# A mixture-of-experts kernel's slot stage rebuilt: first layer transposed, copied weights, eight groups of batches instead of five

## The chip, the core and the metric

One core of a Trainium2 chip. The time is the device time of one execution in microseconds, the median of several runs; less is better. A profiled execution of each kernel gives the busy times, waits and timelines that are quoted.

## What is computed

One transformer block over x of 16 batches x 512 tokens x 128 channels, with adaptive layer norm: each batch has shifts, scales and gates (`sa, ca, ga, sb, cb, gb`) from a small product.

```
h = layernorm(x) * (1 + ca) + sa
x = x + ga * attention(h)          # 16 heads of 8, rope, causal mask
h = layernorm(x) * (1 + cb) + sb
x = x + gb * ffn(h)

ffn: logits = h @ router_w.T + expert_bias          # 160 experts
     probs = sigmoid(logits); top 8 per token
     w = 2.5 * top_w / (sum(top_w) + 1e-9)
     routed = sum over the token's 8 experts e of  w_e * silu(h @ w_gate[e].T) @ w_down[e].T
     shared = silu(h @ w_gate_shared.T) @ w_down_shared.T
     ffn = routed + shared                           # inner width 64
```

## The kernel before

The kernel has two stages. In the first, attention runs batch after batch, four groups of heads per batch (`attend`, 64 calls). Between its matmuls a list of small jobs (`Steps`) puts other work: preparing the next batches, and for a finished batch `project`, then `route` (layer norm, router logits, the top 8 of each token with MAX8 and MATCH_REPLACE8). When all batches of a *group* are routed, `place` gives each chosen (token, expert) pair a slot. Two experts share a *pair* of 128 hidden columns (2 x 64); there are `NC` = 80 pairs. The slots of a pair fill whole blocks of 128. A group of n batches gets `32 n + 80` blocks, so that there are always enough, and the last 8 quads of blocks (6 for a group of one batch) are spare: they run only when they are needed, behind a branch on all engines (`spare_quads`).

GpSimd then scatters the tokens' rows into the group's slots in HBM (`scattering`, indirect DMAs of 128 rows of 512 bytes, 32 per batch). The slots have been cleared before by DMAs from SyncE (`clear`, five in each `attend`).

In the second stage, `Quad` works on four blocks (512 slots) at a time, software pipelined over a loop whose order of stages is written by hand; every engine executes its instructions in that order:

- `load` brings the slots' rows `xs` from HBM, `turn` transposes them on TensorE into the PSUM tile `turn`, and ScalarE copies them to `xT`.
- `up` multiplies each block by its pair's gate weights, which lie in SBUF as `wg` (128 rows, 80 pairs of 128 columns and two router columns). The slots are the stationary operand, so the result has slots on partitions. Which of the pair's two experts a slot belongs to is a mask: a second product adds minus 1e30 (`away`) to the 64 columns of the other expert. ScalarE takes silu into `u` (tile `su`).
- The two router columns give the logit of the slot's expert once more. VectorE adds `shift` into `z`, and `begin_weights` and `end_weights` make the slot's unnormalised weight `w` of it, for two quads at a time, with one small silu (`sz`) on ScalarE.
- `back` transposes `u` again and VectorE copies it to `hT` (tile `hwT`); `down` multiplies by the down weights `wd`, loaded from HBM for each quad, and VectorE writes `y` = product times `w`. `y` goes to the slots' result `yg` in HBM.

Which pair a block belongs to is known only at run time. `numbers` loads the pair's numbers into registers (TENSOR_LOAD, line 768): in `load_down` on SyncE's queue, in `name_up` and `name_down` on TensorE's.

After a group's last quad GpSimd gathers for each block of 128 tokens the eight rows of `yg` (`gathering`, line 950: 8 indirect DMAs per 128 tokens, 32 per batch), and `combine` on VectorE adds the eight, multiplies by the token's normaliser `gr.scale` and by the gate, and adds to the residual `xr`, which already holds the shared expert (`shared_expert`).

Scatters and gathers are not issued freely: `Pacer` puts one at each `PACE_SLOTS` of the model time that `Steps` counts from the matmuls, and a manual dependency lets each wait for the matmul in front of it. `LAG` is the number of gathered blocks that may wait for `combine`; there are `LAG + 2` buffers `got`. Matmuls have line 104, transposes 111, and most VectorE and ScalarE instructions 1212, since helpers record them.

Of the kernel before, what the change touches and what calls it, by code (L numbers as in the profile page):

```python
# [35 lines left out]
GROUPS = (4, 4, 4, 3, 1)  # L36
TOPK = 8
FAR = 1e30
TINY = 1e-30
LAG = 4  # L40

PACE, PACE_SLOTS = 1.3, 0.9
# [28 lines left out]
def block_kernel(ctx: ExitStack, tc: tile.TileContext, t: dict, out: bass.AP):  # L71
# [88 lines left out]
    def load_rest():  # L160
        c.wrout = load("wroutT", [D, E])
        c.wgs = load("wgsT", [D, I])
        c.wds = load("wdsT", [I, D])
        c.bias_p = load("bias_p", [NC, 2])
        c.ones = load("ones", [P, 1])
        c.earlier = load("earlier", [P, P], BF)
        c.many = load("many", [1, P], BF)
        c.pairs = load("pairs", [NC, 2, NC])
        c.spread = load("spread", [NC, 2, E])
        c.table = load("table", [P, 2, NKM])  # L170
# [316 lines left out]
    rows = [tc.dram_tile([P, NBLK, D], FP, name=f"rows{b}") for b in range(NB)]  # L487

    somes = const.tile([1, len(GROUPS)], I32, tag="somes", name="somes")

    class Group:
        def __init__(self, g):
# [4 lines left out]
            self.scale = sb.tile([P, self.tb], FP, tag=f"scale{g}", name="scale")  # L497
            self.idx = sb.tile([P, self.tb, TOPK], I32, tag=f"idx{g}", name="idx")
            self.shift = sb.tile([P, self.nk, 2], FP, tag=f"shift{g}", name="shift")
            self.pid = sb.tile([1, self.nq, 9], I32, tag=f"pid{g}", name="pid")  # L500
            self.some = somes[:, g : g + 1]
            self.away = sb.tile(
                [P, -(-2 * self.nk // P), P], BF, tag=f"away{g}", name="away"
            )
            self.m, self.before = [], []
            self.xg = tc.dram_tile([self.nk * P, D], FP, name=f"xg{g}")
# [13 lines left out]
    def route(gr, i):  # L520
# [40 lines left out]
        yield  # L561

        top = sb.tile([P, NBLK, TOPK], FP, tag="top", name="top")
        for j in range(NBLK):
            vec.max(top[:, j, :], key[:, j, :])
            vec.match_replace(
                out=key[:, j, :], in_to_replace=top[:, j, :], in_values=key[:, j, :], imm_value=1.0
            )
            if j % 2:
                yield  # L570
        m = sb.tile([P, NBLK, E], BF, tag="m", name="m", bufs=max(GROUPS) + 2)
        vec.tensor_scalar(m, key, 0.0, None, ALU.is_gt)
# [13 lines left out]
        yield  # L586

        rs = gr.scale[:, i * NBLK : (i + 1) * NBLK]
        vec.reciprocal(top, top)
        vec.tensor_reduce(rs, top, AX.X, ALU.add, negate=True)  # L590
        vec.tensor_scalar(rs, rs, TOPK_EPS, None, ALU.add)
        vec.reciprocal(rs, rs)
        vec.tensor_scalar(rs, rs, ROUTED, None, ALU.mult)

    def place(gr):
# [41 lines left out]

# [58 lines left out]
        lim = gr.shift[:, :nk, :]  # L696
# [6 lines left out]
        vec.tensor_scalar(lim, lim, 1.0, FAR, ALU.subtract, ALU.mult)  # L703

        flat = tmp([P, 2 * NKM], BF, "flat")[:, : 2 * nk]
        vec.tensor_copy(flat, lim.rearrange("p n a -> p (n a)"))
        yield "o"
        pa = bank([P, -(-2 * NKM // P) * P], BF)
        for n, c0 in enumerate(range(0, 2 * nk, P)):
            k = min(P, 2 * nk - c0)  # L710
            turned(pa[:k, n * P : (n + 1) * P], flat[:, c0 : c0 + k], c.identb)
            vec.tensor_copy(gr.away[:k, n, :], pa[:k, n * P : (n + 1) * P])
        yield "o"
        for a in range(2):
            pl = bank([P, nk])
            mm(pl, c.bias_p[:, a : a + 1].broadcast_to([NC, P]), of)
            vec.tensor_tensor(lim[:, :, a], pl, lim[:, :, a], ALU.add)
            yield "o"
# [40 lines left out]
    class Quad:  # L759
# [17 lines left out]
        ALONE = {"xs": "a", "xT": "b", "su": "a", "wd": "c", "hwT": "b", "y": "a"}  # L777
# [11 lines left out]

        def load_down(self):  # L790
            (p0,) = self.numbers(SP, 0, 1, NC - 4)
            self.wd = self.tile([P, 4, D], "wd", 5)
            nc.sync.dma_start(out=self.wd, in_=t["wdT"][:, bass.ds(p0, 4), :])

        def turn(self):
            pt = now.ps.tile([P, S], FP, tag="turn", name="turn")
# [5 lines left out]
        def name_up(self):  # L802
            self.pids = self.numbers(PE, 1, 4, NC - 1)

        def up(self):

            pu = bank2().rearrange("p a (j n) -> p (a j) n", j=2)
            for j in range(4):
                mm(
                    pu[:, j, 0 : P + 2],  # L810
                    self.xT[:, j * P : (j + 1) * P],
                    wg[:, bass.ds(self.pids[j], 1), :].rearrange("p o n -> p (o n)"),
                    j % 2 == 0,
                    False,
                )
                n, k = divmod(4 * self.q + j, P // 2)
                rows_ = min(P, 2 * self.gr.nk - n * P)
                mm(
                    pu[:, j, 0:P].rearrange("p (a i) -> p a i", a=2),
                    self.gr.away[:rows_, n, :],  # L820
                    c.identb[:rows_, 2 * k : 2 * k + 2].unsqueeze(2).broadcast_to([rows_, 2, I]),
                    False,
                    j % 2 == 1,
                )

            if self.alone or self.q % 2 == 0:
                self.z = self.tile([P, 2, 4, 2], "z", 3)
            else:
                self.z = self.other.z
            vec.tensor_tensor(  # L830
                self.z[:, self.q % 2],
                pu[:, :, P : P + 2],
                self.gr.shift[:, 4 * self.q : 4 * self.q + 4, :],
                ALU.add,
            )
            self.u = self.tile([P, 4, P], "su", 3)
            act.activation(self.u, pu[:, :, 0:P], AF.Silu)

        def begin_weights(self):

            if self.q % 2 == 0 and not self.alone:
                return
            of = slice(self.q % 2, self.q % 2 + 1) if self.alone else slice(0, 2)
            z = self.tile([P, 2, 4], "z1", 3)
            self.w = self.tile([P, 2, 4], "w", 4)
            if not self.alone:
                self.other.w = self.w
            self.s = self.tile([P, 2, 4], "sz", 3)
            z, w = z[:, of], self.w[:, of]
            vec.tensor_tensor(z, self.z[:, of, :, 0], self.z[:, of, :, 1], ALU.max)  # L850
            vec.tensor_scalar(w, z, 0.0, TINY, ALU.is_equal, ALU.mult)
            vec.tensor_tensor(z, z, w, ALU.add)
            vec.reciprocal(w, z)
            act.activation(self.s[:, of], z, AF.Silu)

        def end_weights(self):
            if self.q % 2 or self.alone:
                of = slice(self.q % 2, self.q % 2 + 1) if self.alone else slice(0, 2)
                vec.tensor_tensor(self.w[:, of], self.w[:, of], self.s[:, of], ALU.mult)

        def back(self):
            pt = now.ps.tile([P, S], FP, tag="back", name="back")
            for j in range(4):
                turned(pt[:, j * P : (j + 1) * P], self.u[:, j, :], c.ident)
            self.hT = self.tile([P, S], "hwT", 3)
            vec.tensor_copy(self.hT, pt)
# [4 lines left out]
        def down(self):  # L871
            py = now.ps.tile([P, S], FP, tag="down", name="down")
            for j in range(4):
                mm(
                    py[:, j * D : (j + 1) * D],
                    self.hT[:, j * P : (j + 1) * P],
# [3 lines left out]
            vec.tensor_tensor(  # L880
                y,
                py.rearrange("p (n d) -> p n d", d=D),
                self.w[:, self.q % 2].unsqueeze(2).broadcast_to([P, 4, D]),
                ALU.mult,
            )
# [4 lines left out]
    def spare_quads(gr):  # L890
# [5 lines left out]
        with tc.If(some != 0):  # L896
            for q in range(gr.nq - spare(gr.size), gr.nq):
                quad = Quad(gr, q)
                quad.alone = True
                for stage in ("load", "load_down", "turn", "name_up", "up", "name_down"):  # L900
                    getattr(quad, stage)()
                quad.begin_weights()
# [509 lines left out]
```

## Time and profile before

| what | value |
|---|---|
| median of 3 runs | 1918.97 us (1918.86 to 1922.9) |
| profiled execution | 1925.86 us |
| its span | 1924.1 us |
| mean granted TensorE clock | 0.934 |
| busy: PE, PE weight loads, DVE, ACT, POOL | 1584.2, 1133.7, 1253.8, 826.6, 1117.9 us |
| first and last `turn` of a quad | 974.0, 1794.7 us |
| first scatter, first gather, last gather | 411, 1228, 1915.5 us |

The busy times are sums over the whole span; the stages have different limits, so windows and waits of the slot stage (from 974 us) count for this change. GB/s and the DMA share are means over 16 DMA engines. In a group of instructions, "out<-in" names the tiles.

### The profile page before, as it was taken

How to read it: one execution, taken by the hardware profiler on the slowest of the kernel's cores; microseconds unless marked ns; L12 is line 12 of the kernel's file. 1: busy time of each engine (PE TensorE's matmuls, PEld its weight loads, DVE VectorE, ACT ScalarE, POOL GpSimd, SP SyncE). 2: the span in 40 equal slices, each digit the busy share in tenths (PEclk: the TensorE clock that was granted, in tenths of full speed). 3: DMA queues.
4: the chain of work that ended last, by engine and by line, in shares of the span. 5: the costliest groups of instructions: out<-in, count | busy, mean ns of one | idle time of the engine just before them, and what ended most of it. 6: DMA issues, size and time to landing. Idle time of an engine off the chain costs nothing. (4 is left out here: it accounts for less than half of the span.)

```text
span 1924.1 us, 38397 instructions
## 1 busy us (share of the span) xinstructions
PE 1584.2 (82%) x12683; PEld 1133.7 (59%) x12747; DVE 1253.8 (65%) x3325; ACT 826.6 (43%) x1366; POOL 1117.9 (58%) x1139
## 2 busy tenths in 40 slices
PE   2799999998999989999888887888898878878700
PEld 1355555554555545555468776777788777777600
DVE  2677888887788867787636554546576656666622
ACT  1366666655666556664544332333233323323100
POOL 4001111047775477845657476777777777777776
PEclk8799999998999999999999898999899989999855
DMA  2456555565676667843257676778688878878622
GB/s 83 105 175 201 170 174 170 163 197 177 191 234 188 199 192 219 262 127 117 77 185 244 197 251 203 240 246 275 214 266 272 258 225 272 255 251 254 196 58 57
DMA packets 246678, 377.03 MB, mean 196 GB/s; under 512 B 37604, under 2 KB 136261, under 8 KB 246469
## 3 DMA queue, kind: packets, MB, share of 16 engines
q1 hardware_dynamic: 213700, 307.17, 51.4%
q0 software_dynamic: 32768, 67.17, 12.1%
q8 instruction: 119, 1.95, 0.4%
q14 instruction: 91, 0.74, 0.1%
HBM read 195.15 MB, written 178.26 MB: 194 GB/s over the span
## 5 line engine op out<-in xcount | busy, mean ns | idle before, releaser
L741 POOL DMA_INDIRECT xg<-hs,idx x512 | 493.4, 964 | 284.5 <-issue 95.0
L950 POOL DMA_INDIRECT got<-yg,idx x512 | 491.5, 960 | 156.7 <-issue 123.5
L1212 DVE TENSOR_REDUCE mins<-s 128x2 f32<-128x1024 f32 (+3 forms) x448 | 395.9, 913 | 123.5 <-PE s L104 121.7
L1212 ACT ACTIVATE pT<-s 128x1024 f32<-128x1024 f32 x320 | 323.0, 1021 | 176.7 <-PE s L104 172.3
L104 PE MATMUL s<-wg,xT 128*128 x1520 | 279.6, 307 | 0.6 <-issue 0.6
L104 PEld LDWEIGHTS s<-wg,xT 128*128 128x128 f32 x1520 | 241.6, 200 | 11.3 <-issue 1.2
L111 PE MATMUL turn<-ident,xs 128*128 128x128 f32 x760 | 123.8, 287 | 121.8 <-issue 49.7
L104 PE MATMUL s<-krep,qrep 96*128 96x512 bf16 (+3 forms) x1024 | 197.8, 306 | 31.9 <-DMA qrep<-parts 19.0
L104 PE MATMUL down<-wd,hwT 128*128 x1520 | 206.6, 280 | 3.7 <-DVE y L1212 3.7
L235 POOL TENSOR_TENSOR rot<-rot,three 128x512 f32<-128x512 f32 x32 | 36.8, 1160 | 291.4 <-ACT three L1212 289.4
L104 PE MATMUL s<-qrep,krep 128*128 128x128 bf16 (+3 forms) x960 | 181.6, 299 | 25.3 <-DVE mins L1212 12.3
L104 PE MATMUL av<-pT,v 128*32 128x512 f32 (+3 forms) x2048 | 193.4, 449 | 0.0
L104 PEld LDWEIGHTS down<-wd,hwT 128*128 128x128 f32 x1520 | 190.8, 197 | 4.1 <-DVE y L1212 4.0
L1212 ACT COPY xT<-turn 128x512 f32<-128x512 f32 x190 | 109.8, 578 | 164.8 <-PE turn L111 161.8
L111 PEld LDWEIGHTS turn<-ident,xs 128*128 128x128 f32 x760 | 85.6, 145 | 156.8 <-issue 116.4
L1212 DVE TENSOR_TENSOR z<-s,shift 128x8 f32<-128x8 f32 x190 | 29.6, 156 | 219.3 <-PE s L104 206.5
L104 PEld LDWEIGHTS <-identb 128*128 128x128 bf16 x1280 | 122.0, 100 | 84.9 <-issue 7.0
L104 PE MATMUL s<-identb,away 128*128 128x128 bf16 (+1 forms) x760 | 171.2, 225 | 0.0
L1212 ACT ACTIVATE su<-s 128x512 f32<-128x512 f32 x190 | 113.6, 598 | 129.3 <-DVE z L1212 121.8
L1212 DVE COPY hwT<-back 128x512 f32<-128x512 f32 x190 | 131.0, 689 | 44.2 <-PE back L111 43.6
L1212 DVE TENSOR_TENSOR y<-down,w 128x512 f32<-128x512 f32 x190 | 131.2, 691 | 38.5 <-PE down L104 33.6
L104 PEld LDWEIGHTS <-qrep 96*128 96x128 bf16 x1024 | 83.6, 99 | 119.7 <-issue 95.5
(179 smaller groups left out, 2356.6 us busy)
## 6 DMA issues: line engine op xcount, KB each, us to landing
xg<-zeros SPq DMA_DIRECT2D x228, 256.0 KB
xs<-xg SPq DMA_DIRECT2D x190, 256.0 KB
wd<-in_wdT SPq DMA_DIRECT2D x190, 256.0 KB
yg<-y SPq DMA_DIRECT2D x190, 256.0 KB
krep<-parts SPq DMA_DIRECT2D x64, 288.0 KB
qrep<-parts SPq DMA_DIRECT2D x192, 96.0 KB
parts<-three SPq DMA_DIRECT2D x96, 128.0 KB
yg<-zeros SPq DMA_DIRECT2D x38, 256.0 KB
```

The source lines that it names most:

```text
L104: steps.last = nc.tensor.matmul(out_, lhsT=lhsT, rhs=rhs, start=start, stop=stop).ins
L111: steps.last = nc.tensor.transpose(out_, in_, ident).ins
L235: in_order(getattr(nc.gpsimd, op)(*args).ins)
L741: s = nc.gpsimd.indirect_dma_start(out=gr.xg, out_offset=bass.IndirectOffsetOnAxis(ap=gr.idx[:, NBLK * i + j, k : k + 1], axis=0), in_=h[: ...
L950: s = nc.gpsimd.indirect_dma_start(out=got[:, k, :], out_offset=None, in_=gr.yg, in_offset=bass.IndirectOffsetOnAxis(ap=gr.idx[:, NBLK * i ...
L1212: return getattr(self.engine, op)(*args, **kwargs)
```

## The change

- `GROUPS` goes from (4, 4, 4, 3, 1) to (2, 3, 3, 2, 2, 2, 1, 1), `LAG` from 4 to 3, `PACE_SLOTS` from 0.9 to 0.75.
- `up` has the operands exchanged: the gate weights are stationary and `xT` moves, so the result comes with hidden columns on partitions, as `down` wants it. `back` and `hT` go.
- The stationary weights are copied first: `fetch_up` copies the four blocks' 128x128 weights from `wg` to `wq`, two on ScalarE and two on VectorE, each engine after a register load of its own. `name_up` goes from TensorE.
- The mask is one product per quad: a constant of two rows (`half`) times two rows of the quad's 512 slots (`hide`), which `place` writes to HBM and `load_hide` brings back for two quads at a time.
- The slots' weights go (`z`, `w`, `sz`, `shift`, `away`, the router columns of `wg`). Instead `route` stores the tokens' sigmoid keys and the mask of the chosen eight in HBM (`keys`, `chosen`). In the slot stage a new job `weights(b)` per batch loads them and gives each token's eight weights, in the order of the gathered rows: it builds sortable numbers from the expert's number and 16 bits of the key, takes MAX8, and does so again for the other 16 bits.
- `y` is a plain copy on ScalarE, and `combine` multiplies the eight gathered rows by the weights before it adds them.
- The PSUM banks: `turn` and `up` two each, `down` one; the loop is two turns shorter.

```
-GROUPS = (4, 4, 4, 3, 1)
+GROUPS = (2, 3, 3, 2, 2, 2, 1, 1)
-LAG = 4
-PACE, PACE_SLOTS = 1.3, 0.9
+LAG = 3
+PACE, PACE_SLOTS = 1.3, 0.75
...
         act.activation(key, key, AF.Identity, bias=minus, scale=-1.0)
         yield
+        nc.sync.dma_start(out=keys[b], in_=key)
...
+        nc.sync.dma_start(out=chosen[b], in_=m)
...
+            hide = sb.tile([P, P], BF, tag="hide", name="hide", bufs=2)
+            vec.tensor_copy(hide[:k], pa[:k, n * P : (n + 1) * P])
+            for a in range(2):
+                nc.sync.dma_start(
+                    out=gr.hide[a, c0 * I : (c0 + k) * I].rearrange("(n s) -> n s", s=P),
+                    in_=hide[a:k:2],
+                )
...
+        def fetch_up(self):
+
+            self.wq = self.tile([P, 4, P], "wq", 3)
+            for engine, copy, at in (
+                (mybir.EngineType.Activation, act.copy, 0),
+                (mybir.EngineType.DVE, vec.tensor_copy, 2),
+            ):
+                for j, pid in enumerate(self.numbers(engine, 1 + at, 2, NC - 1), at):
+                    copy(
+                        self.wq[:, j, :], wg[:, bass.ds(pid, 1), :].rearrange("p o n -> p (o n)")
+                    )
...
-            pu = bank2().rearrange("p a (j n) -> p (a j) n", j=2)
+            pu = now.ps.tile([P, S], FP, tag="up", name="up", bufs=2)
             for j in range(4):
+                to = pu[:, j * P : (j + 1) * P]
                 mm(
-                    pu[:, j, 0 : P + 2],
+                    to,
+                    self.wq[:, j, :],
                     self.xT[:, j * P : (j + 1) * P],
-                    wg[:, bass.ds(self.pids[j], 1), :].rearrange("p o n -> p (o n)"),
-                    j % 2 == 0,
+                    j == 0,
                     False,
                 )
...
+            mm(pu, c.half, self.hide, False, True)
+            self.u = self.tile([P, S], "su", 3)
+            act.activation(self.u, pu, AF.Silu)
...
-            vec.tensor_tensor(
-                y,
-                py.rearrange("p (n d) -> p n d", d=D),
-                self.w[:, self.q % 2].unsqueeze(2).broadcast_to([P, 4, D]),
-                ALU.mult,
-            )
+            act.copy(y.rearrange("p n d -> p (n d)"), py)
...
+    def weights(b):
+        while len(weighed) < weighing.index(b):
+            yield
+        key = moe.sb.tile([P, NBLK, E], FP, tag="wkey", name="wkey")
+        nc.sync.dma_start(out=key, in_=keys[b])
+        m = moe.sb.tile([P, NBLK, E], BF, tag="wm", name="wm")
+        nc.sync.dma_start(out=m, in_=chosen[b])
+        yield LATER
+        base = moe.sb.tile([P, NBLK, E], FP, tag="base", name="base")
+        vec.tensor_tensor(base, m, c.high.unsqueeze(1).broadcast_to([P, NBLK, E]), ALU.mult)
...
+        for n, (by, mask) in enumerate(((16, 0x7FFF), (0, 0xFFFF))):
+            vec.tensor_scalar(digit, bits, by, mask, ALU.logical_shift_right, ALU.bitwise_and)
+            vec.tensor_tensor(both, base, digit, ALU.add)
+            yield
+            for j in range(NBLK):
+                vec.max(eight[:, n, j, :], both[:, j, :])
...
+        vec.tensor_tensor(
+            got, got, w[:, j, :].unsqueeze(2).broadcast_to([P, TOPK, D]), ALU.mult
+        )
         for n in (4, 2, 1):
             vec.tensor_tensor(got[:, 0:n, :], got[:, 0:n, :], got[:, n : 2 * n, :], ALU.add)
...
-    for i in range(-3, len(quads) + 7):
+    for i in range(-3, len(quads) + 5):
         for stage, q in (
             ("load", i + 3),
-            ("load_down", i - 3),
-            ("name_up", i - 1),
-            ("name_down", i - 5),
-            ("end_weights", i - 4),
-            ("begin_weights", i - 3),
+            ("load_hide", i),
+            ("load_down", i - 1),
+            ("fetch_up", i),
             ("turn", i),
             ("up", i - 2),
-            ("back", i - 4),
-            ("down", i - 6),
+            ("name_down", i - 3),
+            ("down", i - 4),
```

## The prediction

> **What bounds the kernel now.** I read the page's slices first, then windows over the slot stage, the engines' timeline of one quad, and last the waits.
>
> ```profile
> span 1924.1 us, 38397 instructions
> POOL 4001111047775477845657476777777777777776
> DMA  2456555565676667843257676778688878878622
> ```
>
> Up to about 974 us the kernel does attention (TensorE nearly always busy), from there the slots, from 1815 us only gathers. GpSimd starts to scatter in the ninth slice and is busy at 7 of 10 from slice 25 to the end.
>
> ```profile
> 1000.00:1010.00 10.00, 10.00 (x71) 7.72 (x70) 3.81 (x11) 5.03 (x8) 7.56 (x9) 1.00 0.96 331
> ...
> 1400.00:1500.00 100.00, 87.85 (x752) 81.19 (x750) 71.80 (x203) 35.09 (x73) 76.15 (x79) 1.00 0.86 273
> ...
> 1800.00:1850.00 50.00, 15.43 (x88) 11.82 (x87) 21.50 (x52) 2.67 (x6) 38.11 (x40) 0.63 0.42 122
> 1850.00:1900.00 50.00, 0.00 (x0) 0.00 (x0) 10.98 (x27) 0.00 (x0) 37.81 (x41) 0.50 0.23 58
> ```
>
> The columns after the time are PE, PE's weight loads, DVE, ACT and POOL, then clock, DMA share and GB/s. GpSimd issues about 79 to 80 gathers in 100 us with work beside it and 41 in 50 us with none: one per 1.25 us (0.94 busy, 0.30 between) is its natural rate. DMA can go to 331 GB/s for 10 us and has held 273 for 100 us.
>
> ```profile
> 1523.00 0.63 PE L111 MATMUL turn<-ident,xs 128*128 128x128 f32 x4 [0.81 <-ACT su L1212]
> 1523.46 0.39 PE L104 MATMUL s<-wg,xT 128*128 x2
> ...
> 1524.75 0.61 PE L111 MATMUL back<-ident,su 128*128 128x128 f32 x4
> ...
> 1525.19 1.06 PE L104 MATMUL down<-wd,hwT 128*128 x8
> ...
> 1526.08 0.60 PE L111 MATMUL turn<-ident,xs 128*128 128x128 f32 x4
> ```
>
> From start to start a quad costs TensorE 0.46 (turn) + 1.29 (up with masks) + 0.44 (back) + 0.89 (down) = 3.08 us. The 190 quads, however, take (1815 - 974) / 190 = 4.43 us each. The waits say where the rest goes:
>
> ```profile
> ACT sz L1212 <- DVE z L1212: 206.4, 88, 7.8
> PEld turn L111 <- issue: 116.4, 96, 6.9
> ...
> L768 PEldq TENSOR_LOAD <-pid x380: 332/1004/2452, 974.0 to 1807.9; - x190
> ...
> L892 ACTq TENSOR_LOAD <-somes x5: 278/479/756, 1186.2 to 1811.1; - x5
> L892 DVEq TENSOR_LOAD <-somes x5: 304/312/555, 1187.3 to 1815.9; - x5
> ```
>
> ScalarE stands in `sz` behind VectorE's weights and combines, so the next `xT` leaves the only `turn` bank late; and TensorE's sequencer loads block numbers twice per quad, 1.0 us each, more than its queued matmuls always cover. So the slot stage is bound by a chain PE, DVE, ACT with GpSimd close to full beside it, and the end by the gathers left over: (1924 - 1815) = 109 us.
>
> **The change, part by part.** All sums are against the profiled execution (span 1924.1, 1925.9 with what lies around it); the median shown, 1919.0, lies 7 us lower, so 7 is taken off at the end.
>
> *Number of quads.* A group of n batches has 32n + 80 blocks, so 8n + 20 quads, less 8 spare ones (6 for n = 1). Before: 44 + 44 + 44 + 36 + 22 = 190. After: 28, 36, 36, 28, 28, 28, 22, 22 = 228. That is 38 quads more, at any price.
>
> *TensorE per quad.* `back` goes (0.44). Up takes down's form, four fp32 products of 128 columns: 0.89; the eight mask instructions become one bf16 product of 512 columns (0.22 at the 128-column masks' rate of 0.055). Sum 0.46 + 0.89 + 0.22 + 0.89 = 2.46. One of two register loads remains, 1.0 us, covered by the down matmuls queued behind the sequencer; uncovered it costs what two did now, some 0.5. The shared expert (about 2.6 us per batch, 16 / 228) adds 0.18; at the stage's mean clock of 0.95 (the windows' clock column, averaged) that is 2.64 / 0.95 = 2.78 us.
>
> *ScalarE per quad.* Out: `sz` (0.21 per two). In: `y` and two weight copies. The profile's rows:
>
> ```profile
> L1212 ACT COPY xT<-turn 128x512 f32<-128x512 f32 x190 | 109.8, 578 | 164.8 <-PE turn L111 161.8
> L1212 ACT ACTIVATE su<-s 128x512 f32<-128x512 f32 x190 | 113.6, 598 | 129.3 <-DVE z L1212 121.8 <-ACT xT L1212 4.5 <-DVE w L1212 1.5
> ```
>
> 0.578 + 0.598 + 0.58 for `y` + two copies. No copy of 128x128 from SBUF is in the trace: the nearest row is `gate` (PSUM source) at 265 ns, the upper bound the normalisation's 128-column rows at 483. I take 0.27. The sum is 2.30 us, plus a register load of 0.48 (0.28 to 0.76) that starts while `y` still runs: 2.3 to 2.8.
>
> *VectorE.* Out per quad: `z` 0.16, five small ones (0.44), `hwT` 0.69, `y` 0.69. In: two copies (0.22 to 0.30 each by `away` and `xr<-xr,got`), 0.5 taken. In per batch: four products of 1024 columns, 1.22 each from the rows' slope, 4.9; and `weights`, two casts-and-adds of 640 columns and eight MAX8 at 0.32, about 8 us. With the old combine's 8.3 and the shared expert's 1, 22 us per batch: 2.0 us per quad in all, below TensorE, but in lumps of 3 us in front of the weight copies. Up uses these two turns later, which covers 5 us.
>
> *DMA.* Each quad moves 3 x 256 KB. 228 quads 179 MB, some 100 scatters left plus 512 gathers at 64 KB 40 MB, per batch 3 x 256 KB + 480 KB (`keys`, `chosen`) 20 MB: 239 MB. At 300 GB/s, between the 273 held and the 331 seen, 797 us. The Trainium skill ("SBUF — State Buffer", A bandwidth-pool intuition that's wrong) gives 358 GB/s from HBM to a core; by it 668 us, and DMA would not bind. The trace holds less already at a share of 0.96, so I take 300.
>
> *GpSimd.* About 100 scatters and 512 gathers at 1.25 us are 765 us after the switch. The skill's rule ("SBUF — State Buffer", SBUF: two separate sides) speaks against the change: VectorE's fp32 copies within SBUF lock the port through which GpSimd writes its descriptors. By the rule 456 copies of 0.25 could add up to 114 us. The row: a gather's median is 944 ns and its mean 960 with the `got` sums beside it, 2%, or 15 us. I take 15 and keep the 114 for the range.
>
> *SP.* `load_hide` is one issue per two quads; `keys` and `chosen` are two in and two out per batch at 0.4, and wait for ACT's `key` and DVE's `m` with q/k fetches queued behind them, four groups ahead; cost taken as nothing, and a few us a batch if that lead is gone. Clears grow from 266 to 348. Five per attention group go (320), so 28 are left for the switch: 28 x 0.38 = 11 us of SP ahead of the first `xs`.
>
> *Attention.* Three more placings, smaller masks, no scale: -5 to +20, +5 taken. With the clears the first turn is at 990 instead of 974.
>
> *Spare blocks.* Each branch makes its quad 9.6 to 10.4 us long instead of 3.8, and the clock is halved after it: 8 us. Seven lie inside the stage: 56 (before four).
>
> *Tail.* After the last down, 32 gathers: 3.5 + 40 + 9 (as now from the last gather) + 1.5 = 54 instead of 109, provided GpSimd has no backlog. It hasn't: by the seventh group's end, about 1715, it has had time for 580 of the 548 due.
>
> *Sum.* Bytes give (797 - 56) / 233 turns = 3.18 us, TensorE 2.78, ScalarE 2.3 to 2.8, GpSimd 780 / 233 = 3.35 with branches' time included, 3.1 without. Where four are this close no one of them runs free, so 3.25. 990 + 233 x 3.25 + 56 + 54 = 1857, median 1850. Equal to now at X = (1924 - 1100) / 233 = 3.54.
>
> **The rivals.**
>
> *GpSimd is the floor.* The quads run at 2.8 as TensorE alone allows: 990 + 652 + 56 + 54 = 1752, and GpSimd ends at 990 + 780 + 9 = 1779; median 1772. For it: no DMA wait among the SP's. Against it: 239 MB in 710 us is 337 GB/s, more than the best ten microseconds of now.
>
> *ScalarE becomes the serial engine: slower.* Its queue takes all of a quad's evacuations in order, and now a register load and two copies ahead of `xT`. If the load isn't hidden (0.76), copies cost 0.48 and each of five waits 0.06, the turn is 0.76 + 0.97 + 1.76 + 0.30 = 3.8 us: 990 + 885 + 56 + 54 = 1985, median 1978. It decides from 3.54. For it: `y` has only two buffers and needs `yg` to land while DMA is at 0.9. Against: a load of this kind began 25 ns after `su` did and ran beside it. DMA sustaining under 271 GB/s ends at the same place.
>
> *The gain is eaten by quads alone.* The chain through VectorE was not what cost 4.43, X stays at 3.54: 1924, no change.
>
> **How the numbers follow.** 3.05 to 3.45 per turn has 0.45 (1803 to 1897); GpSimd's floor 0.20; 3.45 to 3.52 0.08; no change 0.04; slower 0.23. So faster 0.73, same 0.04, slower 0.23. A difference under 0.2% can't be told here from none. The range 1768 to 1955 leaves out the best of the second case and the worst of the slow one; the likeliest case alone is 1803 to 1897.
>
> **What would show it.** Right: 228 `xT` at 3.2 to 3.3 us, no `back`, DMA at 290 to 310 GB/s over the slot stage, last down near 1800 and 32 to 40 gathers after it, first gather near 1100 instead of 1228, first scatter near 290 instead of 411. Wrong: ScalarE above 85% in the slot stage or `y` waiting for `yg` (the slower rival); TensorE idle for `wq` from VectorE (its lumps); gathers above 1.3 us each (the port rule); the first turn after 1010.

## The result, and the profile after

The changed kernel takes 1993.34 us (median of 4 runs, 1989.1 to 1997.8) against 1918.91 for the kernel before: a ratio of 1.0385 [1.0356, 1.0415], so it is slower, and the prediction of 1850 us has the wrong sign. The profiled execution has a span of 1993.5 us, 69 more than before.

Two rows of the changed kernel's page, the busy tenths of GpSimd and DMA in 40 slices:

```profile
POOL 4001117713775567766736757677777774757636
...
DMA  3456646756766676667688688888787888888871
```

GpSimd begins two slices earlier than before (first scatter at 304 us instead of 411), but then it is not steadily at 7: it has holes (a 3 in slice 21, a 4 and a 5 in slices 34 and 36, a 3 in slice 39), where the kernel before shows 7 in nearly every slice of the last third. The windows (PE, weight loads, DVE, ACT, POOL, then clock, DMA share, GB/s):

```profile
1400.00:1500.00 100.00, 78.46 (x503) 64.87 (x503) 56.24 (x158) 50.56 (x116) 77.13 (x76) 0.88 0.78 249
1700.00:1800.00 100.00, 87.76 (x605) 74.17 (x606) 53.00 (x154) 60.22 (x142) 63.70 (x64) 0.91 0.87 285
1950.00:1993.00 43.00, 0.00 (x0) 0.00 (x0) 12.87 (x24) 0.00 (x0) 26.43 (x28) 0.50 0.19 50
```

In the first, GpSimd gathers back to back and TensorE is at 78%, at a clock of 0.88; in the second TensorE does better and GpSimd issues only 64 gathers. The first turn of the quads comes at 1022 us instead of 974, the last down at 1940 instead of 1815, and the tail after it is 53 us.

Of the waits of the stage of quads (engine, line, what was waited for: us in total, times, longest):

```profile
DVE got L1217 <- DMA got<-yg,idx: 62.1, 21, 6.8
POOL got L961 <- SPq L861: 60.6, 3, 26.4
...
PE o L110 <- DMA hr<-rows: 33.6, 7, 6.5
...
PE up L103 <- DMA hides<-hide: 24.6, 14, 3.0
PE up L103 <- DVE wq L1217: 24.6, 14, 5.4
PE turn L110 <- DMA xs<-xg: 23.5, 3, 21.3
```

VectorE waits for gathered rows, TensorE for weight copies on VectorE and for loads that come late (`hr` of the shared expert, the mask's `hides`), and GpSimd stands three times for up to 26 us at the branch of the spare blocks (L861), with nothing to gather. SyncE, which issues the loads, stands 78 us in front of the store `out`, which waits for `combine`:

```profile
SPq L985 <- DVE xr L1217: 77.7, 14, 11.9
```

One case in which these waits hang together: `combine` waits 2.8 us for gathered rows and begins at 1418.6, the copies to `wq` stand behind it on VectorE, and SyncE stands from 1411 to 1422 in front of `out`, with `hides` behind it. TensorE meanwhile:

```profile
1422.79 1.22 PE L103 MATMUL up<-xT,wq 128*128 128x128 f32 x4 [3.41 <-DVE wq L1217]
1425.94 0.58 PE L103 MATMUL up<-hides,half 2*128 2x512 bf16 x1 [1.94 <-DMA hides<-hide]
...
1429.14 1.06 PE L110 MATMUL turn<-ident,xs 128*128 128x128 f32 x4
1429.99 1.92 PE L103 MATMUL up<-xT,wq 128*128 128x128 f32 x8
```

From 1422.8, at the end of the first of these waits, to 1433.0 the granted clock is 0.5. And one of GpSimd's holes:

```profile
1917.87 0.95 POOL L961 DMA_INDIRECT got<-yg,idx  x1 [0.30 <-PE down L103]
1945.23 0.94 POOL L961 DMA_INDIRECT got<-yg,idx  x1 [26.42 <-SPq L861]
```

A group's gathers exist only when its last quad and its branch are through. GpSimd had emptied its list before that, and the next gather comes right behind the branch.

**An account by GpSimd's line.** From the traces: the time of the first turn, the scatters then left and the 512 gathers at 1.25 us each (the median from start to start in these runs), GpSimd's idle time between them (each distance over 2 us, less 1.25), and as the rest the wait for the first of them, the short gaps and some 8 us behind the last gather:

| run | first turn | scatters left | (scatters + 512) x 1.25 | idle | rest | end |
|---|---|---|---|---|---|---|
| before | 974 | 197 | 886 | 34 | 30 | 1924.1 |
| after | 1022 | 142 | 818 | 119 | 35 | 1993.5 |
| e16 (pace, stores, clears) | 1002 | 142 | 818 | 38 | 40 | 1898.2 |
| e17 (the same, old groups) | 974 | 195 | 884 | 48 | 43 | 1948.7 |
| e18 (the same, 3, 4, 4, 4, 1) | 991 | 196 | 885 | 87 | 35 | 1998.7 |

Such a sum comes out for any engine; it tells something here because little of it is idle time. In the kernel before GpSimd idles for 34 of 950 us behind the first turn, so that its line, and not the quads, sets the end. In the changed kernel the quads set it in part, through the 119 us in which GpSimd waits for them. The change puts 55 more scatters under attention (-69 us), comes 48 us later to the first turn, and lets GpSimd stand 85 us longer: that and 5 us of rest are the 69 us.

And TensorE's side, the stage from first turn to last down, cut into idle (gaps over 0.15 us), what the halved clock costs (half of the busy time in stretches of granted clock 0.5), and the rest, its own work at full clock:

| run | stage | quads | idle | halved clock | own work | per quad |
|---|---|---|---|---|---|---|
| before | 842 | 190 | 135 | 32 | 674 | 3.55 |
| after | 919 | 228 | 149 | 65 | 705 | 3.09 |
| e16 | 834 | 228 | 92 | 36 | 706 | 3.10 |
| e17 | 671 | 190 | 62 | 27 | 582 | 3.07 |

A quad is 13% cheaper, but there are 20% more of them.

### The profile page after: what moved, and what is told of

Read it like the earlier page. It is cut to its first block, busy times and chain, and to the rows that moved or that the text cites. A ratio compares the mean times of both kernels' runs of the same rounds, so it can differ in the third digit from the quotient of the medians.

```text
span 1993.5 us, 39230 instructions
## 1 busy us (share of the span) xinstructions
PE 1650.2 (83%) x12248; PEld 1129.7 (57%) x12248; DVE 1188.0 (60%) x3153; ACT 1080.0 (54%) x2031; POOL 1144.1 (57%) x1139
## 5 line engine op out<-in xcount | busy, mean ns | idle before, releaser
L103 PE MATMUL down<-wd,su 128*128 x1824 | 280.0, 300 | 30.5 <-DMA yg<-y 5.9
L103 PEld LDWEIGHTS down<-wd,su 128*128 128x128 f32 x1824 | 236.2, 202 | 114.3 <-issue 51.6
L103 PE MATMUL up<-xT,wq 128*128 128x128 f32 x1824 | 268.5, 293 | 31.1 <-DVE wq L1217 24.6
L103 PEld LDWEIGHTS up<-xT,wq 128*128 128x128 f32 x1824 | 245.8, 208 | 34.7 <-DVE wq L1217 27.6
L1217 ACT COPY y<-down 128x512 f32<-128x512 f32 x228 | 133.5, 586 | 184.4 <-PE down L103 121.4
L1217 DVE COPY wq<-wg 128x128 f32 x456 | 92.2, 250 | 235.4 <-PE up L103 146.6
L103 PE MATMUL s<-qrep,krep 128*128 128x512 bf16 (+3 forms) x1024 | 194.8, 303 | 33.5 <-DVE mins L1217 13.0
L1217 ACT ACTIVATE su<-up 128x512 f32<-128x512 f32 x228 | 136.3, 598 | 99.6 <-PE up L103 98.7
L1217 DVE TENSOR_TENSOR got<-got,w 128x1024 f32<-128x1024 f32 x64 | 78.3, 1224 | 99.3 <-DMA got<-yg,idx 96.2
L1217 ACT COPY wq<-wg 128x128 f32 x456 | 114.2, 296 | 40.8 <-issue 11.9
```

What stands on the lines that cost most here:

```text
L103: steps.last = nc.tensor.matmul(out_, lhsT=lhsT, rhs=rhs, start=start, stop=stop).ins
L1217: return getattr(self.engine, op)(*args, **kwargs)
```

## The experiments

E1 to E12 ran on three chips (E1 to E4, E5 to E8 and E9 to E12 on one each) on which the kernel before takes 2195 to 2199 us, below called the slower chips; the result above and E13 to E18 are from faster chips, on which it takes 1919 to 1920. Each ratio is to runs of the kernel before on the same chip. Edits are shown shortened.

**E1 to E4: pace, the store of the output, clears, groups, one at a time.** Theory Q was: one gather per 0.75 us of planned time asks for more than GpSimd gives; combines on VectorE and the store `out` on SyncE then stand in front of copies and loads.

```
-PACE, PACE_SLOTS = 1.3, 0.75                # E1, again as E7
+PACE, PACE_SLOTS = 1.3, 1.1
-   if j == NBLK - 1: nc.sync.dma_start(out=out[b]..., in_=xr)    # E2
+   if j == NBLK - 1: late_outs.append((turn + 6, b, xr))         #  issued six turns later
-   if n % 3 == 1 and clears:                # E3
+   if (n % 3 == 1 or n == 6) and clears:
-GROUPS = (2, 3, 3, 2, 2, 2, 1, 1)           # E4
+GROUPS = (4, 4, 4, 3, 1)
```

> Only PACE_SLOTS goes from 0.75 to 1.1. Theory Q (queues behind the gathers): the program asks for a gather about every 0.8 us, GpSimd gives one per 1.25, so `combine` on VectorE waits for rows, and the weight copies on VectorE and `out` on SyncE's queue stand behind it. Slower pacing takes the backlog away: VectorE's waits for `got` in the slot stage fall from 62 us to under 20, SyncE's for `xr` from 78 to under 25, the slot stage (first turn to last down) from 919 us to 820 to 850; more gathers are left for the end, time 1920 to 1960. Theory D (the bytes of 228 quads): the slot stage stays over 890 us, since as much is moved, and the tail grows: 2000 to 2040. Theory S (ScalarE serial): as D.

> `out` of a batch is issued on SyncE's queue six turns of the loop later, nothing else. Theory Q: SyncE no longer waits for `xr` (78 us to under 10), loads are not late and TensorE's waits for `hr`, `xs` and `hides` (33.6, 23.5 and 24.6 us) fall to under half, but the weight copies still stand behind `combine`: slot stage 919 to 870 to 895, time 1945 to 1975. Theories D and S: SyncE's order does not matter, 1983 to 2003.

> Six clears in each attention group instead of five, so that none of the 28 is left for the switch. If they delay the first slots' loads: first turn from 1022 to 998 to 1005, TensorE's wait for `xs` there (21 us) gone, time 1970 to 1980. Rival: the clears cost the attention stage what they save at the switch (DMA or SyncE time in both), first turn within 5 us of 1022, time 1985 to 2000.

> The changed kernel with the groups of before, (4, 4, 4, 3, 1): 190 quads instead of 228. If the new quad is good and the groups lost the time: first turn under 1000, 190 quads at 4.0 us or less, but 64 us later first gather; GpSimd then ends at about first gather 1230 + 640 + 9: 1880 to 1930. If the new quad itself lost it (theories D, S): 190 quads over 4.4 us and over 1950.

Measured, ratios to before with their 95% intervals: E1 0.9953 [0.9932, 0.9974], E2 1.0717 [1.0670, 1.0763], E3 1.0634 [1.0589, 1.0679], E4 1.0146 [1.0098, 1.0195]. Against the unaltered change (E5, 1.0753) the later output store gives nothing that counts. The times expected were for a faster chip; as shares of E5, E1 gains more than Q gave it (2 to 4%), E2 as little as D and S said, E3 and E4 what was expected of the clears and of the groups. E3 brings the first turn to 1093 us, where E1 and E2 on the same chip have 1109 and 1105 (the last clear is issued at 1009 instead of 1104 and 1100), and gains about 1%. E4 has its first turn at 1048 (before, on a chip as slow: 1056): the later start comes from the groups. The pace is the largest single term here (E1 is 7.4% under E5), and the groups are the second: taken back at the old pace (E4) they gain 5.6%.

**E5 to E8: the unaltered change as control, and three ways to take a queue out of the path.**

```
-   xr, gate, w = residual[b]                # E6: combine works on a fixed tile of zeros
+   xr, gate, w = residual[b]; got = still   #     (leaves out the use of the gathered rows;
                                             #     one gather tile fewer)
-   for engine, copy, at in ((Activation, act.copy, 0), (DVE, vec.tensor_copy, 2)):     # E8
-       for j, pid in enumerate(self.numbers(engine, 1 + at, 2, NC - 1), at): copy(...)
+   for j, pid in enumerate(self.numbers(Activation, 1, 4, NC - 1)): act.copy(...)
```

> The changed kernel unaltered, as the control for the other runs of this call. Its ratio to the kernel before was 1.0385 with 1993 us, and its stage of quads lasted 919 us (1022 to 1940). Theory Q (combines and stores queue behind gathers that are late) says nothing new here; both theories expect a ratio of 1.03 to 1.05. If the chip of this call is as slow as that of the first experiments (2195 us for the kernel before), the ratio should lie between those of the runs with only the store or the clears moved (1.063 to 1.072) and 1.04.

> Leaves out that the combine uses the gathered rows: it multiplies and sums a fixed tile of zeros instead, with the same instructions of the same sizes, while all 512 gathers still run (four gather tiles instead of five). So VectorE never waits for a gather, and the store of a batch never waits for one either. Theory Q: most of the stalls vanish; TensorE's idle time in the slot stage falls from about 149 us to 60 to 80 and the stage from 919 to 830 to 850 us, the total to 0.95 to 0.98 of the kernel before. Theory D (228 quads move too many bytes, 256 KB three times each, which DMA can't carry faster): the stage keeps 890 us or more, ratio 1.02 to 1.04. Theory S (ScalarE's serial queue): also unchanged.

> As the first experiment, a gather asked for per 1.1 us of planned time instead of 0.75, now beside the unaltered changed kernel on one chip. Q: fewer stalls in the stage but more gathers left at the end, net 3 to 5% faster than the changed kernel, ratio to before 0.98 to 1.01. D and S: gathers are only moved to the end, so it is slower than the changed kernel by 1 to 3%.

> All four weight copies of a quad on ScalarE, so nothing of VectorE lies between a quad's turn and its up products. Q: up's waits for the copies (about 52 us in TensorE's two rows) go, ScalarE rises by 2 x 0.30 us per quad (137 us, to about 70 to 75% busy), VectorE still stands behind gathers but only the store, the shared expert and the weights are late; stage 870 to 910 us, 1 to 4% faster than the changed kernel. S: ScalarE becomes the bound, 0.6 us per turn more, 137 us longer stage, ratio to before 1.10. D: no change.

Measured: E5 1.0753 [1.0729, 1.0777], E6 1.0719 [1.0695, 1.0743], E7 0.9924 [0.9896, 0.9952], E8 1.0843 [1.0813, 1.0872]. E5 is above all that was expected of it: the change loses more on the slower chips. Theory Q falls there: nothing waits for a gathered row in E6, and the stage is 1186 us instead of 1195. In E8 neither Q's gain nor S's 1.10 came. E7 repeats E1: 7.7% against E5, more than Q gave it, with the same 622 scatters and gathers inside the stage and 53 us behind it. So it isn't that gathers were moved to the end. GpSimd's idle time, by the account above, falls from 397 to 205 us with the pace; with the clears (E3) or the stores (E12) moved it stays at 378 and 384. Counted in blocks of eight turns in which GpSimd has no holes, E5 has about 4 gathers and scatters per turn and turns of about 6 us, E7 about 3 and 4.5. The turn grows with the number of gathers that the pace puts beside it.

How it looks there, in E6's timeline:

```profile
1733.71 0.38 PE L103 MATMUL up<-hides,half 2*128 2x512 bf16 x1
...
1743.37 0.94 POOL L962 DMA_INDIRECT got<-yg,idx  x1 [0.30 <-issue]
1745.48 0.36 DVE L1221 COPY wq<-wg 128x128 f32 x2 [9.73 <-remote]
...
1746.82 0.60 ACT L1221 ACTIVATE su<-up 128x512 f32<-128x512 f32 x1 [10.68 <-remote]
...
1747.95 0.80 PE L103 MATMUL down<-wd,su 128*128 x2 [13.85 <-ACT y L1221]
```

`su` needs only the product that ended near 1734.1 (the profile models the ends of matmuls), and begins 12.7 us later; TensorE, VectorE and ScalarE all stand while GpSimd issues gather after gather, and go on when its row of gathers is over. The profile names nothing as the releaser ("remote"). Two of E5's waits of this kind:

```profile
DVE wq L1217 <- remote: 151.9, 30, 12.0
...
ACT su L1217 <- remote: 133.1, 29, 8.7
```

This is not what happens in the result. In the slot stage ScalarE, VectorE and GpSimd wait 645 us for "remote" in E5, 147 in E7 and 179 in the kernel before (E9), all on slower chips; in the result, in the kernel before on its chip and in E13 to E18 it is not there once. On the other hand VectorE's waits for gathered rows, 62 us in the result's stage and 0.5 in that of the kernel before, are 0.7 us in E5: E6 took away a wait that was not there. So it excludes theory Q for the slower chips only, and the 7.7% is the worth of the pace on them.

**E9 to E12: where the slower chips lose, the quads without gathers, and the stores.**

```
-pacer = Pacer(PACE_SLOTS, scatter, gather)  # E10 (after) and E11 (before)
+pacer = Pacer(PACE_SLOTS, scatter)          #   all 512 gathers follow the last down
-    nc.sync.dma_start(out=self.gr.yg[...], in_=y)     # E12
+    nc.scalar.dma_start(out=self.gr.yg[...], in_=y)
```

> The kernel before, unaltered, for its profile on the chip on which the experiments run, where it took 2195 to 2199 us instead of 1919. It tells where the extra 276 us lie. If the chip delays all loads, attention and quads grow by the same share (14%: attention 974 to 1110, quads 842 to 960). If only the stage with gathers suffers, attention stays near 1000 to 1030 and the quads take about 1050.

> The changed kernel with no gather beside the quads: all 512, and with them the combines, come after the last down. The stage of quads then shows what 228 quads cost by themselves. Theory P (the quads are cheap, as forecast, and the gathers beside them are what costs): stage 228 x 2.9 to 3.2 plus 8 branches x 8 = 725 to 795 us, followed by 512 x 1.25 = 640 us of gathers, total about 2500 us. Theory D (bytes and SyncE's own issues bound the turn): stage 228 x 3.8 + 64 = 930 us or more, total 2650 us or more.

> The same for the kernel before: no gather beside the quads. By P its 190 quads take 190 x 3.7 to 4.1 plus 5 x 8 = 745 to 820 us, so about as long as the 228 of the changed kernel, and the whole takes 2500 us too: the change then wins nothing on the quads and pays for its eight groups. By D the stage is 190 x 3.8 + 40 = 760 us, shorter than the changed kernel's by 150 us or more.

> The changed kernel with the store of a quad's y issued from ScalarE's queue, right behind the copy it waits for, instead of from SyncE's, where xs, hides and wd of later quads stand behind it (SyncE stood 149 us in that wait). Theory H (head of SyncE's line: the loads are late because stores stand in front of them): TensorE's idle time falls by a third or more, the stage by 60 to 120 us, ratio to before 1.02 to 1.05 where the changed kernel had 1.0753 on this chip. Against H: less than 1% from the changed kernel, since the prefetch of three quads covers the wait, or slower by up to 3% by the issue time of 228 stores on ScalarE[...].

Measured: E9's first turn is at 1056 us, its stage 1045: attention is 8% longer than in the profile of before on a faster chip, the quads 24%. E10 1.2054 [1.1971, 1.2138] with a stage of 792 us, E11 1.1887 [1.1843, 1.1930] with 836, E12 1.0656 [1.0618, 1.0694]. One window of E10, with no gather beside the quads:

```profile
1500.00:1600.00 100.00, 95.38 (x713) 83.34 (x713) 12.29 (x68) 71.64 (x170) 0.00 (x0) 0.97 0.84 269
```

The same window of E11:

```profile
1500.00:1600.00 100.00, 83.42 (x712) 78.80 (x712) 48.55 (x139) 31.48 (x63) 0.00 (x0) 0.97 0.65 204
```

The changed kernel's stage is within theory P's range and far below D's 930; that of the kernel before is 16 us above P's. Alone, 228 new quads are 44 us faster than 190 old ones; TensorE is 95% busy. P's totals of 2500 us are exceeded by 111 to 150: behind the last down the gathers took 731 us in E10, where 640 were expected. E10 also takes the combines, the weights and the shared expert of most batches out of the stage. Everything beside the quads then costs the change 1195 - 792 = 404 us, the kernel before 1045 - 836 = 209. The stores (E12) are worth 0.9% against E5, not the 2 to 5% of theory H.

**E13 to E16: what of a gather it is, and the way out.**

```
-    out=got[:, k, :], in_=gr.yg                           # E13, on top of E6
+    out=got[:, k, 0:16], in_=gr.yg.rearrange("r (k d) -> (r k) d", d=16)
-    s = nc.gpsimd.indirect_dma_start(out=got[:, k, :], ...).ins    # E14
+    s = nc.gpsimd.memset(got, 0.0).ins
-PACE, PACE_SLOTS = 1.3, 0.9                               # E15, in the kernel before
+PACE, PACE_SLOTS = 1.3, 1.1
 E16: the edits of E1, E3 and E12 together
```

> As the run in which the combine did not use the gathered rows (stage of quads 1186 us, ratio 1.0719), and besides every gather fetches 64 bytes per row instead of 512 (leaves out seven eighths of each row, from other addresses); number of gathers, rows and instructions unchanged. Theory W (the bytes of the gathers crowd out the other transfers): the stage falls to 800 to 900 us. Theory B (it is the indirect DMAs as instructions, back to back, during which the other engines' signals or issues stand): stage 1130 to 1190 us, as before.

> Each of the 512 gathers is replaced by a fill of the gather tile by GpSimd (1024 columns, about 1 us; leaves out the gathering, so the sums are of zeros), at the same places and the same pace. Theory B (indirect DMAs): the quads run as without gathers, stage 790 to 860 us, and the total about 1990 to 2060 us. Theory G (any work of GpSimd that is back to back with LAG blocks of slack holds up VectorE and through it the quads): stage 1000 us or more.

> The kernel before with one gather per 1.1 us of planned time instead of 0.9. If the slower pace is worth something of itself, the kernel before gains from it as well: stage of quads 1045 to about 960 to 1000 us, ratio 0.96 to 0.98. If the pace was right for the old quad and only became too fast with the shorter planned turn of the new one, no gain: ratio 0.99 to 1.02 (fewer stalls, more gathers left at the end).

> The changed kernel with three edits together: one gather per 1.1 us of planned time, the stores of y from ScalarE's queue, six clears per attention group. From their single effects on this chip (pace -7.6%, stores -1%, clears 13 to 16 us at the switch): 2364 x 0.924 x 0.99 - 15 = 2148 us, ratio to before 0.977. If the stores' issue on ScalarE matters once the pace is right, 0.99.

Measured: E13 1.0080 [1.0049, 1.0111], E14 1.0150 [1.0109, 1.0192], E15 1.0498 [1.0468, 1.0527], E16 0.9892 [0.9852, 0.9932]. E13's stage is 850 us and E14's 882, where the changed kernel has 919 on such a chip, so bytes and rows of the gathers cost something here; but E13 takes bytes and the wait for rows away at once, E14's fills also come every 1.01 us instead of 1.25, and both expectations were made for the slower chips. They do not settle what in a gather it is. In E13 TensorE's wait for `wq` falls from 24.6 to 3.1 us and that for `hides` from 24.6 to 15.3, as theory Q has it. E15 lies outside both expectations: the slower pace is no gain of itself, the kernel before loses 5% by it, because 171 gathers instead of 80 are left behind its last down (225 us, from 1793 to 2018; the stage itself is 20 us shorter). E16 is 1.1% faster than before, less than the 2.3% expected but clear of its interval, and so 4.7% faster than the changed kernel. GpSimd's row of its page:

```profile
POOL 4001115731767376776674767677777777777776
```

Two of its windows:

```profile
1400.00:1500.00 100.00, 86.65 (x619) 72.88 (x618) 66.34 (x182) 59.14 (x147) 77.40 (x75) 0.97 0.91 299
1700.00:1800.00 100.00, 89.25 (x629) 73.76 (x628) 60.51 (x170) 60.05 (x149) 77.13 (x76) 0.97 0.92 304
```

GpSimd is at 7 up to the end with no hole over 5 us, at the same 75 to 76 gathers per 100 us as in the first window of the changed kernel, but TensorE beside it is at 87 to 89% instead of 78, the clock at 0.97 instead of 0.88, and DMA reaches 299 to 304 GB/s. VectorE's waits for rows are 11 us in the stage instead of 62, and TensorE's gaps ahead of `up` sum to 4 us instead of 56. So on the faster chips gathers back to back don't of themselves bring TensorE down to 78%. The traces point to theory Q: at the faster pace the program has the sum of the rows in VectorE's order before GpSimd has fetched them, and copies and loads stand behind it. No run on these chips changes that alone: how much of E16's gain is the pace and how much the stores and clears was not run apart, and `LAG` was never changed back.

**E17 and E18: the groups taken back.** E16 with `GROUPS = (4, 4, 4, 3, 1)` and with `(3, 4, 4, 4, 1)`.

> As the run with slower pace, stores on ScalarE and six clears (ratio 0.9892, first turn 1002, stage 834 us), but with the groups (4, 4, 4, 3, 1) of before, so 190 quads. If the groups are what the change loses by: first turn 970 us, TensorE's own work in the stage 190 x 3.1 = 590 us instead of 706, and the bound is GpSimd: about 170 scatters and 512 gathers at 1.27 us = 866 us, so an end near 970 + 866 + 50 = 1886 us, ratio 0.975 to 0.99. If the smaller groups were what fed GpSimd earlier and so paid for themselves: 1920 us or more, ratio 1.00 to 1.02.

> The same with groups of 3, 4, 4, 4 and 1 batches, 190 quads too, so that scatters and gathers start one batch earlier. If GpSimd's start is the bound: 20 to 40 us less than with (4, 4, 4, 3, 1), ratio 0.96 to 0.98; if not, the same within 1%.

Measured: E17 1.0169 [1.0141, 1.0197], E18 1.0441 [1.0421, 1.0460]. At this pace and on these chips the groups are not what the change loses by: with the old ones it is 2.8% slower. (At the old pace on a slower chip, E4, they were.) The rows of TensorE and GpSimd on E17's page:

```profile
PE   2799999998899989999898999989888987121100
...
POOL 4001111157674477737567466767777777777776
```

A window of it behind the last down:

```profile
1700.00:1900.00 200.00, 23.69 (x64) 13.13 (x64) 98.97 (x233) 5.77 (x12) 152.98 (x155) 0.50 0.26 79
```

The quads are through at 1645 us, 191 us before those of E16, and the whole is 51 us longer (1949 to 1898): 304 us of gathers follow. By the account: first turn 28 us earlier, but 53 more scatters left (66 us) and 13 more of idle and rest. E18 came out as neither of its expectations: it begins 17 us later than E17 and stands 39 us longer, in which is one hole of 49 us at 1049 us, a group's scatters not yet there.

## Why the prediction was wrong, step by step

**Right.** *The quad*, nearly. Undisturbed, as in this stretch of TensorE's timeline in E16, it takes 2.73 us from turn to turn:

```profile
1401.47 0.60 PE L110 MATMUL turn<-ident,xs 128*128 128x128 f32 x4
1401.90 1.06 PE L103 MATMUL up<-xT,wq 128*128 128x128 f32 x8
1402.89 0.38 PE L103 MATMUL up<-hides,half 2*128 2x512 bf16 x1
1403.21 1.16 PE L103 MATMUL down<-wd,su 128*128 x8
1404.20 0.60 PE L110 MATMUL turn<-ident,xs 128*128 128x128 f32 x4
```

The forecast had 2.46: up and down 0.99 from start to start instead of 0.89, the mask 0.32 instead of 0.22. *The copies*, costed without a row of their own, were right:

```profile
L1217 ACT COPY wq<-wg 128x128 f32 x456 | 114.2, 296 | 40.8 <-issue 11.9 <-ACTq L766 7.6 <-DVE got L1217 3.4
...
L1217 DVE COPY wq<-wg 128x128 f32 x456 | 92.2, 250 | 235.4 <-PE up L103 146.6 <-issue 26.6 <-ACT wq L1217 15.2
```

0.27 and 0.25 were taken, 0.296 and 0.250 measured. ScalarE did not become serial (50 to 60% in the windows). *Bytes*: 239 MB forecast, 244 moved within the stage. *Tail*: 54 forecast, 53 measured. *First scatter*: 290 forecast, 304 measured; the first gather, at 1159 instead of 1100, was not. The port rule (the Trainium skill, "SBUF — State Buffer", SBUF: two separate sides): a gather's mean is 1000 ns against 960, 20 us over 512, near the 15 taken from the row and far from the estimate of up to 114 by the rule. With all copies on ScalarE (E8) the mean is 979, against 996 in E5. *DMA's rate*: 300 GB/s was forecast as what DMA can hold; E16 moved 292 over its stage, so the 266 of the changed kernel are not DMA's limit.

**Wrong: what bounds the stage, and the turn.** In the forecast's own terms the first turn came 32 us later, a turn took (919 - 56) / 233 = 3.70 us instead of 3.25 (+105), and the tail fitted. The first step, "bound by a chain PE, DVE, ACT with GpSimd close to full beside it", had the order wrong: in the kernel before GpSimd is idle for 34 of 950 us, so a cheaper chain alone could bring the end forward by little more, and the forecast has GpSimd as no more than one of four rates that the turn might take. Read by its line, the forecast of 1857 had 990 for the first turn, (100 + 512) x 1.25 = 765 and so 102 left for idle and rest. Measured: 1022, 818 and 154. That is +32, +53 and +52, the 136 us by which it missed.

- *"With the clears the first turn is at 990"* (+32). Attention's last group ends at 1000.5 instead of 971.7: the placings of eight groups cost 29 us, not 5. In E17, with the groups of before, it ends at 971.8. Of the clears 21 came after attention and the first turn waited for `xs` up to 1022; in E16 none did, and the first turn is at 1002. So the clears cost some 18 us, not 11: fewer were left than forecast, but they were issued 0.80 us apart, where 0.38 was taken (a median of 0.46 already in the trace of before).
- *"About 100 scatters"* (+53). 142 were left at the first turn. The trace of before had 197; the earlier start takes 55 off, no more.
- *The pace was not costed at all* (with the next step, most of the +52). The diff lowers `PACE_SLOTS` from 0.9 to 0.75 and `LAG` from 4 to 3, and the prediction says nothing of either. The quads slow down while there is something to gather; then GpSimd has emptied its list and stands until the slowed quads finish the next group. Idle grew from 34 to 119 us. The pace alone is worth 7.7% on the slower chips (E7 against E5), where the waits are of another kind; with stores and clears it turns 1.0385 into 0.9892 on the faster ones (E16), idle 38 us. There the pace was not run by itself.
- *"SP cost nothing"* and *"up uses these two turns later, which covers 5 us"*. Both covers fail: TensorE waits 25 us for `wq` from VectorE, as the prediction's own signs of being wrong had it, 25 for `hides` and 34 for `hr`. In E16 the first two are 2 us each and the third 15. On the slower chips, where these waits are small (in E5 2 us for `hr` and at most 2 for `wq`), moving the copies (E8, 0.8% longer than E5) or the stores (E12, 0.9% shorter) did little; on the faster ones neither was moved by itself.
- *TensorE 2.64 per quad with the shared expert, at full clock* is 3.09: 0.27 of it are the longer products, the rest placing of later groups, short pauses and the branches. Its own work rises by 31 us over that of before, where the forecast's numbers (2.46 x 228 against 3.08 x 190) have it fall by 24. (The "eight mask instructions" of the old quad are four products, 760 for 190 quads; the forecast's sum doesn't use the number.) It is not what bounds E16: E17 has 124 us less of it and is slower.

**The rivals.** *GpSimd is the floor* had the right mechanism at too low a sum, 1772; with 1022, 818 and 35 us of rest it is 1874 us even without any idle. *ScalarE serial* came out near the time measured (1978) by luck: ScalarE was not the serial engine. One of its reasons is in the trace, `y` waiting 47 us for `yg` to land, but TensorE's gaps put down to it are 6 us. *No change* needed a turn of X = 3.54; it was 3.70.

**Open.** On the slower chips, why a close row of indirect DMAs holds up the other engines; the waits for gathered rows, the copies and the stores are excluded there as the main cause (E6, E8, E12). On the faster ones, how the loss divides between pace, `LAG`, stores and clears; rows and bytes of the gathers together are worth 62 us (E13 against the changed kernel, 1931.5 to 1993.5), not told apart.

## What to carry to other kernels

Before costing the turns of a loop, write down the line of the engine that has the most fixed work left (first start, count times its period, idle, end), since a cheaper loop body moves nothing on it except its idle time. A pace is part of a change like any instruction: asking an engine for more per turn than it gives doesn't make it earlier; here those who use its results stood in line for them, and it was idle afterwards. Smaller groups paid at the slower pace, through the scatters that they moved under attention and not through the quads; at the faster pace, on a slower chip, they cost 5.6%. And an experiment explains a result only where the same waits are seen: look for the result's waits in the trace of the experiment before using it.

## What the runs showed of the hardware

- One and the same program differs by 14% between the chips used here (1919 and 2198 us for the kernel before), and not evenly: 8% in attention, 24% in the quads. The ratio of the two kernels moves with it, from 1.0385 to 1.0753.
- On the chips with the longer times TensorE, VectorE and ScalarE stand together for some 9 us, and TensorE for up to 14, while GpSimd issues gathers at 1.25 us (E6); the profile names no releaser. On the chips with the shorter times no such wait is in the slot stage of any trace.
- Idle time of a few us of TensorE was paid twice: the granted clock is 0.5 for 10.2 us behind the wait of 3.4 us shown above, and `turn` takes 0.85 us from start to start (at 1429 us) instead of 0.43. In the changed kernel the halved clock costs 65 us beside 149 idle, on a slower chip 172 beside 322 (E5).
- A gather of 64-byte rows takes GpSimd as long as one of 512-byte rows: mean 1023 ns (E13) and 1000.
